# Layer norm with tokens on partitions in the attention stage of a four-layer network

## The chip, the cores and the metric

The kernel runs on one core of a Trainium2 chip. The metric is the device time of one execution in microseconds (us). A core has a matrix engine (PE, with weight loads listed as PEld), a vector engine (DVE), an activation engine (ACT), a general engine (POOL) and a queue that issues transfers (SP). Each works through its own instructions in order, and they wait for each other through semaphores. Matrix products are written to PSUM, eight banks of 2 KB per partition.

## The reference, cut to what matters

Four layers follow each other: a Mamba block, a depthwise convolution with a GELU network, a linear attention with a quantised network, and a Fourier layer with a quantised network. The change lies in layer 2 and at the start of layer 3. There are 4 images of 4096 tokens with 96 channels.

```
t = t + attn(ln(t))            # layer 2
t = t + ffn_quantised(ln(t))
t = t + fourier(ln(t))         # layer 3
t = t + ffn_quantised(ln(t))

def ln(v):                     # over the 96 channels of a token
    return (v - mean(v)) / sqrt(var(v) + 1e-5)
```

The attention has no softmax, so for a head it is q (k^T v) with biases. A batch therefore needs the Gram matrix of its normalised tokens (with a row of ones for the biases), from which one 97x96 matrix follows, by which every token is multiplied.

## The kernel before

The stream `t` stays in SBUF as [96 channels, 16384 tokens] in float32. Function `layer2` works on blocks of 512 tokens (MB), 8 per batch (NB), n = 32 in all. It writes the order of all its instructions by hand: one loop over iterations j, in which each step handles a block that is some iterations behind. Nothing is reordered later, so what stands first in an iteration is first in its engine's queue.

There are 72 blocks to normalise: 0 to 31 for the attention, 32 to 63 for the quantised network (FFN), and 64 to 71 for the first batch of the Fourier layer, written to `h3`. All go through `norm_steps`. Step `center` multiplies by a centring matrix (L1084, to PSUM tile `xc_ps`) and squares the result on ACT (L1086). Step `scale` multiplies the squares by a matrix of ones (L1090, tile `v_ps`), which sums them over the channels and leaves the sum on all partitions, and takes Ln and Exp on ACT (L1092, L1093). Step `norm` multiplies on DVE (L1096).

For the attention, `turn` then transposes a normalised block in four pieces of 128 tokens (L1131) and ACT copies them to SBUF (L1133); `products` adds them to the Gram matrix (L1141). At the end of a batch, `weights` gives five small steps: copies on ACT, small products on PE (L1147) and a mask on DVE (L1165). They are handed out over the following iterations, two at a time. Step `out` multiplies a block by the batch's matrix (L1179) and adds to `t` on DVE (L1181), 15 iterations after the block was centred.

The FFN steps `hidden` (three products L1236, three ACT copies L1238, three DVE operations L1239, a POOL cast L1240) and `project` (L1246, two DVE operations L1248 and L1250, a POOL addition L1252) run in the same loop, three and five iterations after the block is centred. The tile of `project` shares its PSUM bank with that of `out`.

The loop's core, with the order within an iteration:

```python
lag = NB + 3
for j in range(2 * n + NB + 2):
    scale(j - 1); center(j)
    norm(j - 2, ...)
    products(j - 4)        # at a batch's end: steps = weights(b)
    turn(j - 3)
    for f in steps[:2]: f()
    out(j - 4 - lag)
    project(j - n - 5)
    hidden(j - n - 3)
```

Two neighbours of the change appear in the text because they do similar things. Layer 1 normalises with tokens on partitions: DVE statistics (L1006, L1007), Ln and Exp on 16 values per partition (L1011, L1012), DVE scaling (L1020), transposes back (L1025). Layer 0 does so with ACT operations (L371, L377, L378, L384), transposes L390 and copies L401. In the Fourier layer, L1376 is an ACT operation with a scale and a bias per partition, read from PSUM. L594, L488 and L940 are transposes on PE in layers 0 and 1.

Of the kernel before, what the change touches and what calls it, by code (L numbers as in the profile page):

```python
# [9 lines left out]
F32 = mybir.dt.float32  # L10
# [3 lines left out]
AF = mybir.ActivationFunctionType  # L14
ALU = mybir.AluOpType
# [3 lines left out]
B, C, HW, L = 4, 96, 64, 4096  # L19
NT = B * L  # L20
T = 1024
NSC = L // T
MB = 512
# [79 lines left out]
class Net:  # L103
# [972 lines left out]
    def norm_steps(self, t, wk, psum):  # L1076
# [20 lines left out]

        return center, scale, norm

    def layer2(self, t, h3):
        tc, nc = self.tc, self.nc
        NB = L // MB
        n = B * NB
        engines = {mybir.EngineType.PE, mybir.EngineType.DVE, mybir.EngineType.Activation, mybir.EngineType.Pool}
        with ExitStack() as ctx:
            wk = ctx.enter_context(tc.tile_pool(name="l2w", bufs=1))
            psum = ctx.enter_context(tc.tile_pool(name="l2p", bufs=1, space=PSUM))
            tc.keep_in_program_order(nc.scalar.preload_act_table_set(ACT_EXP_LN))  # L1110
            ctx.enter_context(tc.manual_schedule(engines=engines))
            center, scale, norm = self.norm_steps(t, wk, psum)
            hidden, project, xq = self.ffn_steps("f2", t, wk, psum, ("ht", "gram", "small", "o"))
            nc.gpsimd.memset(h3[C:], 1.0)

            hs = []
            for k in range(2):
                h = wk.tile([C + 1, L], F32, name=f"h{k}")
                nc.gpsimd.memset(h[C:], 1.0)
                hs.append(h)  # L1120
            ht, gram, g = {}, {}, {}

            def block(i):
                b, s = divmod(i, NB)
                return hs[b % 2][:, s * MB : (s + 1) * MB]

            def turn(i):
                h = block(i)
                ps = psum.tile([128, 4, C + 1], F32, name="ht_ps", tag="ht")
                for d in range(4):  # L1130
                    nc.tensor.transpose(ps[:, d], h[:, d * 128 : (d + 1) * 128], self.ident[: C + 1, : C + 1])  # L1131
                ht[i] = wk.tile([128, 4, C + 1], F32, name="ht", tag="hts", bufs=2)
                nc.scalar.copy(ht[i], ps)  # L1133

            def products(i):
                b, s = divmod(i, NB)
                if s == 0:
                    gram[b] = psum.tile([C + 1, C + 1], F32, name="gram", tag="gram")
                h = ht.pop(i)
                for d in range(4):  # L1140
                    nc.tensor.matmul(  # L1141
                        gram[b], h[:, d], h[:, d], start=s == 0 and d == 0, stop=s == NB - 1 and d == 3
                    )

            def small(w, x, rows, name):
                ps = psum.tile([C + 1, C], F32, name="small_ps", tag="small")[:rows]
                nc.tensor.matmul(ps, w, x, start=True, stop=True)  # L1147
                r = wk.tile([C + 1, C], F32, name=name, tag=name, bufs=2)[:rows]
                return r, ps

            def weights(b):

                m = {}

                def one():
                    m["g"] = wk.tile([C + 1, C + 1], F32, name="grams", tag="grams")
                    nc.scalar.copy(m["g"], gram.pop(b))

                def two():
                    m["p"], ps = small(m["g"], self.wkv[:, :C], C + 1, "gk")  # L1160
                    nc.scalar.copy(m["p"], ps)

                def three():
                    m["m"], ps = small(self.wkv[:, C:], m["p"], C, "kv")
                    nc.vector.tensor_mul(m["m"], ps, self.mask)  # L1165

                def four():
                    m["w"], ps = small(m["m"], self.wff, C, "mw")
                    nc.scalar.copy(m["w"], ps)

                def five():
                    g[b], ps = small(self.wqt, m["w"], C + 1, "g")
                    nc.scalar.copy(g[b], ps)

                return [one, two, three, four, five]

            def out(i):
                ps = psum.tile([C, MB], F32, name="o_ps", tag="o")
                nc.tensor.matmul(ps, g[i // NB], block(i), start=True, stop=True)  # L1179
                td = t[:, i * MB : (i + 1) * MB]  # L1180
                nc.vector.scalar_tensor_tensor(td, ps, self.v("bff"), td, ALU.add, ALU.add)  # L1181

            lag = NB + 3
            steps = []
            for j in range(2 * n + NB + 2):
                if 0 <= j - 1 < 2 * n + NB:
                    scale(j - 1)
                if j < 2 * n + NB:  # L1190
                    center(j)
                i = j - 2
                if 0 <= i < n:
                    norm(i, block(i)[:C])
                elif n <= i < 2 * n:
                    norm(i, xq(i - n), saturate=False)
                elif i >= 2 * n:
                    norm(i, h3[:C, (i - 2 * n) * MB : (i - 2 * n + 1) * MB])
                if 0 <= j - 4 < n:
                    products(j - 4)  # L1200
                    if (j - 4) % NB == NB - 1:
                        steps = weights((j - 4) // NB)
                else:
                    for f in steps[:1]:
                        f()
                    steps = steps[1:]
                if 0 <= j - 3 < n:
                    turn(j - 3)
                for f in steps[:2]:
                    f()  # L1210
                steps = steps[2:]
                if 0 <= j - 4 - lag < n:
                    out(j - 4 - lag)
                if 0 <= j - n - 5 < n:
                    project(j - n - 5)
                if 0 <= j - n - 3 < n:
                    hidden(j - n - 3)
# [464 lines left out]
```

## Time and profile before

| quantity | value |
|---|---|
| median of 4 runs | 3830.27 us (3827.86 to 3833.89) |
| profiled execution | 3833.89 us, span 3832.0 us |
| mean granted TensorE clock | 0.895 |
| busy: PE, DVE, ACT, POOL | 84%, 78%, 71%, 67% of the span |
| attention and its FFN, with the Fourier layer's first norm | 2923.6 to 3192.2 us, 268.6 us |
| of it, up to the first FFN block's iteration | 111.3 us |

The profiled execution is the slowest of the four, 3.6 us over their median. The shares are averages over stages with different limits: layer 0 alone takes the first two thirds of the span, and its POOL work says nothing on attention. So the stretch from 2923.6 us on is to be read by itself, in the windows by stage and in the timeline, where the start-to-start distances on one engine show what a step costs. PE's matrix products are pipelined, and the end of a product is modelled, so its listed duration is longer than its start-to-start distance. A float32 product over 512 columns is listed as two records.

### The profile page before, as it was taken

To read this page: it belongs to the slowest core of one execution; us is meant where nothing else is said; L and a number is where in the kernel's file an instruction comes from. 1 tells how busy PE (TensorE), PEld (TensorE's weight loads), DVE (VectorE), ACT (ScalarE), POOL (GpSimd) and SP (SyncE) were. 2 spreads that over 40 slices of the span, in tenths; PEclk is the share of its full clock that TensorE was granted. 3 is DMA by queue.
4 is the path that set the end of the run, shared out by engine and by line. 5 is a ranking of instruction groups with operands and counts; after the bars stand their busy time and mean duration, and the time that the engine had idled before them with its cause. 6 is when DMAs were issued, how large, how long until landed. Compare 5 with 4: busy or idle time off the path is not lost. (4 is left out here: it accounts for less than half of the span.)

```text
span 3832.0 us, 46555 instructions
## 1 busy us (share of the span) xinstructions
PE 3227.6 (84%) x15326; PEld 1474.3 (38%) x15326; DVE 2989.4 (78%) x2644; ACT 2718.9 (71%) x5456; POOL 2568.5 (67%) x922
## 2 busy tenths in 40 slices
PE   7888888888888888888888888657799998899988
PEld 3333333233323332333233323226544534666643
DVE  5999989999999999999999999952573384444649
ACT  6788788877887888778877887631345686666557
POOL 1988889888888898888888988832001064544527
PEclk8998899889998999899989887657899999999989
DMA  7566665656565656565666565556200000011101
GB/s 192 150 149 164 160 160 144 169 150 161 136 169 149 165 136 167 152 160 140 166 153 162 138 165 150 132 142 205 75 1 0 1 1 6 19 35 34 37 9 58
DMA packets 171642, 446.61 MB, mean 117 GB/s; under 512 B 48756, under 2 KB 50750, under 8 KB 168064
## 3 DMA queue, kind: packets, MB, share of 16 engines
q1 hardware_dynamic: 171400, 443.64, 44.6%
q8 instruction: 121, 1.98, 0.2%
q14 instruction: 121, 0.99, 0.1%
HBM read 369.97 MB, written 73.50 MB: 116 GB/s over the span
## 5 line engine op out<-in xcount | busy, mean ns | idle before, releaser
L648 POOL TENSOR_TENSOR hs<-hs,crep 128x2048 f32<-128x2048 f32 x384 | 1598.9, 4183 | 213.6 <-DVE hs L643 129.0
L610 ACT ACTIVATE da<-ddb,nega 128x1024 f32<-128x1024 f32 x576 | 657.7, 1147 | 191.9 <-DVE hs L643 181.5
L643 DVE TENSOR_TENSOR_SCAN hs<-da,state,rep 128x1024 f32<-128x1024 f32 x288 | 667.8, 2337 | 59.0 <-PE rep L594 42.9
L665 PE MATMUL y<-hs,sel_r 128*32 128x512 f32 x3072 | 458.2, 680 | 75.7 <-POOL hs L648 75.7
L621 POOL TENSOR_TENSOR up<-udb,brep 128x1024 f32<-128x1024 f32 x192 | 452.0, 2361 | 69.8 <-DMA udb<-ud 59.6
L594 PE MATMUL rep<-ident,uta 128*128 128x128 f32 x1536 | 244.9, 311 | 161.8 <-DVE hs L643 161.7
L507 ACT ACTIVATE uta<-delta,bt 128x192 f32<-128x192 f32 x1024 | 379.0, 442 | 1.1
L643 DVE TENSOR_TENSOR_SCAN hs<-dap,state,up 128x1024 f32<-128x1024 f32 x144 | 336.7, 2338 | 44.7 <-ACT dap L610 44.7
L643 DVE TENSOR_TENSOR_SCAN hs<-da,state,u 128x1024 f32<-128x1024 f32 x144 | 338.1, 2348 | 15.5 <-DVE u L636 0.5
L287 PE MATMUL ps<-n,w_x 97*64 97x512 f32 x1536 | 346.8, 599 | 1.5 <-ACT n L401 1.5
L594 PEld LDWEIGHTS rep<-ident,uta 128*128 128x128 f32 x1536 | 198.6, 159 | 268.0 <-DVE hs L643 148.0
L610 ACT ACTIVATE dap<-ddb,nega 128x1024 f32<-128x1024 f32 x192 | 214.0, 1115 | 102.0 <-DVE hs L643 101.4
L599 PE MATMUL rep<-dbl,sel_b 32*128 32x512 f32 x768 | 246.5, 720 | 29.7 <-DVE hs L643 28.7
L636 DVE TENSOR_TENSOR u<-udb,rep 128x1024 f32<-128x1024 f32 x192 | 235.7, 1228 | 39.4 <-DMA udb<-ud 13.7
L1240 POOL CAST hq<-y 128x1536 fp8e5<-128x1536 f16 x64 | 94.0, 1468 | 218.8 <-issue 122.6
L287 PE MATMUL ps<-dbl,dtw 103*64 103x512 f32 x384 | 172.9, 945 | 74.6 <-ACT dbl L441 74.6
L636 DVE TENSOR_TENSOR rep<-udb,rep 128x1024 f32<-128x1024 f32 x192 | 231.9, 1208 | 0.0
L643 DVE TENSOR_TENSOR_SCAN hs<-da,rep 128x1024 f32<-128x1024 f32 x96 | 216.8, 2277 | 15.0 <-PE rep L594 9.8
L665 PEld LDWEIGHTS y<-hs,sel_r 128*32 128x32 f32 x3072 | 68.5, 116 | 381.2 <-POOL hs L648 192.9
L287 PEld LDWEIGHTS ps<-n,w_x 97*64 97x64 f32 x1536 | 109.9, 137 | 232.4 <-issue 205.1
L479 POOL TENSOR_TENSOR delta<-delta,xc 128x1536 f32<-128x1536 f32 x31 | 106.5, 3437 | 93.1 <-DMA dd<-delta 80.0
L1379 POOL TENSOR_TENSOR av<-av,ec 128x780 f32<-128x780 f32 x32 | 58.8, 1836 | 133.2 <-ACT av L1376 133.2
(276 smaller groups left out, 6220.5 us busy)
## 6 DMA issues: line engine op xcount, KB each, us to landing
ddb<-dd SPq DMA_DIRECT2D x768, 128.0 KB
udb<-ud SPq DMA_DIRECT2D x768, 128.0 KB
crep<-cd SPq DMA_DIRECT2D x512, 128.0 KB
dd<-delta SPq DMA_DIRECT2D x64, 384.0 KB
band<-in_band SPq DMA_DIRECT2D x24, 1024.0 KB
ud<-delta SPq DMA_DIRECT2D x62, 384.0 KB
brep<-cd SPq DMA_DIRECT2D x128, 128.0 KB
x<-in_x SPq DMA_DIRECT2D x32, 384.0 KB
```

The source lines that it names most:

```text
L287: nc.tensor.matmul(ps[rows], w[:, 64 * p : 64 * p + 64], rhs[:, at.start + shift : at.stop + shift], start=k == 0, stop=k == len(ws) - 1, ...
L479: (nc.gpsimd if k else nc.vector).tensor_mul(m["du"], m["delta"], m["xc"])
L507: nc.scalar.mul(m["uta"][:, q, :, 32 * s4 : 32 * s4 + 32].rearrange("t (p j) d -> t p j d", p=3), m["udt"][:, :, q].rearrange("t p (j d) - ...
L594: nc.tensor.transpose(x[:, q * 128 : q * 128 + 128], made[k]["uta"][:, q, 2 * h + j], self.ident)
L599: nc.tensor.matmul(x[:, at], sel_b[rows, g], made[k]["dbl"][rows, at], start=True, stop=True)
L610: nc.scalar.activation(da, made[k]["dd", h, j], AF.Exp, scale=nega[:, col : col + 1])
L621: nc.gpsimd.tensor_mul(up, made[k]["ud", p][:, j], made[k]["brep", GP])
L636: nc.vector.tensor_mul(u, made[k]["ud", h][:, j], x)
L643: nc.vector.tensor_tensor_scan(hs[:, 1:], made[k].pop(("da", t)), u, st, ALU.mult, ALU.add)
L648: nc.gpsimd.tensor_mul(hs[:, :, :T], hs[:, :, 1:], twice(made[k]["crep", g]))
L665: nc.tensor.matmul(made[k]["y", p][row : row + 32], sel_r, made[k]["hs", p, g][:, j, at], start=False, stop=True, skip_group_check=True,)
L1240: nc.gpsimd.tensor_copy(q, y2, saturate=False)
```

## The change

For blocks 0 to 31 and 64 to 71 the norm is made with tokens on partitions, in a new function `token_norm`. Step `turn` transposes a block of `t` into PSUM in four pieces, and DVE takes mean and variance of each token (`bn_stats`, `bn_aggr`). Step `root` takes Ln and Exp on ACT of 4 values per partition, and minus mean times root on DVE. Step `times` scales and shifts on ACT from PSUM to an SBUF tile with tokens on partitions, whose column of ones is set once. Step `back` transposes it and copies the block on ACT to where the channels are on partitions. The Gram matrix is taken from the SBUF tile directly, so the former transposes of the normalised block and their copy go. Blocks 32 to 63 keep the old steps. `products` runs two blocks behind instead of four, and `out` 13 iterations after the block's first step.

```diff
+    def token_norm(self, wk, tile_of, back_of):
...
+        kept = [wk.tile([128, 4, C + 1], F32, name=f"nt{k}") for k in range(3)]
+        for k in kept:
+            nc.gpsimd.memset(k[:, :, C:], 1.0)
+        def turn(i, x):
+            ps = xt[i] = tile_of(i)
+            for d in range(4):
+                nc.tensor.transpose(ps[:, d], x[:, d * 128 : d * 128 + 128], self.ident[:C, :C])
+            m = mv[i] = wk.tile([128, 4, 2], F32, name="tmv", tag="tmv", bufs=3)
+            for d in range(4):
+                st = wk.tile([128, 6], F32, name="tst", tag="tst", bufs=4)
+                nc.vector.bn_stats(st, ps[:, d])
+                nc.vector.bn_aggr(m[:, d], st)
+        def root(i):
+            r = rs[i] = wk.tile([128, 2, 4], F32, name="trs", tag="trs", bufs=3)
+            nc.scalar.activation(r[:, 0], mv[i][:, :, 1], AF.Ln, bias=self.eps)
+            nc.scalar.activation(r[:, 0], r[:, 0], AF.Exp, scale=-0.5)
+            nc.vector.scalar_tensor_tensor(r[:, 1], mv.pop(i)[:, :, 0], -1.0, r[:, 0], ALU.mult, ALU.mult)
+        def times(i):
...
+            for d in range(4):
+                nc.scalar.activation(
+                    n[:, d, :C], x[:, d], AF.Identity, scale=r[:, 0, d : d + 1], bias=r[:, 1, d : d + 1]
+                )
+        def back(i, out):
+            ps = back_of(i)
+            for d in range(4):
+                nc.tensor.transpose(ps[:, d * 128 : d * 128 + 128], nt[i][:, d, :C], self.ident)
+            nc.scalar.copy(out, ps)
...
+            turn, root, times, back, ht = self.token_norm(
+                wk,
+                lambda i: psum.tile([128, 4, C], F32, name="xt_ps", tag="xc", bufs=3),
+                lambda i: psum.tile([C, MB], F32, name="tp_ps", tag=("v", "ht")[i % 2]),
+            )
-            def turn(i):
-                h = block(i)
-                ps = psum.tile([128, 4, C + 1], F32, name="ht_ps", tag="ht")
-                for d in range(4):
-                    nc.tensor.transpose(ps[:, d], h[:, d * 128 : (d + 1) * 128], self.ident[: C + 1, : C + 1])
-                ht[i] = wk.tile([128, 4, C + 1], F32, name="ht", tag="hts", bufs=2)
-                nc.scalar.copy(ht[i], ps)
-            lag = NB + 3
+            lag = NB + 5
-            for j in range(2 * n + NB + 2):
...
+            for j in range(total + 3):
                 i = j - 2
                 if 0 <= i < n:
-                    norm(i, block(i)[:C])
+                    back(i, block(i)[:C])
+                elif 2 * n <= i < total:
+                    a = (i - 2 * n) * MB
+                    back(i, h3[:C, a : a + MB])
+                if n <= j - 1 < 2 * n:
+                    scale(j - 1)
+                elif token_block(j - 1):
+                    root(j - 1)
+                if n <= j < 2 * n:
+                    center(j)
+                elif token_block(j):
+                    turn(j, t[:, j * MB % NT : j * MB % NT + MB])
+                if token_block(j - 1):
+                    times(j - 1)
+                if n <= i < 2 * n:
                     norm(i, xq(i - n), saturate=False)
-                if 0 <= j - 4 < n:
-                    products(j - 4)
...
+                if 0 <= j - 2 < n:
+                    products(j - 2)
...
-                if 0 <= j - 3 < n:
-                    turn(j - 3)
...
-                if 0 <= j - 4 - lag < n:
-                    out(j - 4 - lag)
+                if 0 <= j - lag < n:
+                    out(j - lag)
```

More of the change, by code (lines that the diff above doesn't have):

```diff
@@ L1098, in norm_steps @@
         return center, scale, norm
+    def token_norm(self, wk, tile_of, back_of):
+        nc = self.nc
+        xt, mv, rs, nt = {}, {}, {}, {}
+        kept = [wk.tile([128, 4, C + 1], F32, name=f"nt{k}") for k in range(3)]
[16 more added lines that the diff above has]
+        def times(i):
+            n = nt[i] = kept[i % 3]
+            x, r = xt.pop(i), rs.pop(i)
+            for d in range(4):
[7 more added lines that the diff above has]
+            nc.scalar.copy(out, ps)
+        return turn, root, times, back, nt
     def layer2(self, t, h3):
@@ L1120, in layer2 @@
                 hs.append(h)
-            ht, gram, g = {}, {}, {}
+            gram, g = {}, {}
+            turn, root, times, back, ht = self.token_norm(
[3 more added lines that the diff above has]
+            )
             def block(i):
@@ L1181, in out, with token_block @@
                 nc.vector.scalar_tensor_tensor(td, ps, self.v("bff"), td, ALU.add, ALU.add)
-            lag = NB + 3
+            lag = NB + 5
             steps = []
-            for j in range(2 * n + NB + 2):
[L1188 to L1191, printed above, removed]
+            total = 2 * n + NB
+            def token_block(i):
+                return 0 <= i < n or 2 * n <= i < total
+            for j in range(total + 3):
                 i = j - 2
                 if 0 <= i < n:
-                    norm(i, block(i)[:C])
-                elif n <= i < 2 * n:
-                    norm(i, xq(i - n), saturate=False)
-                elif i >= 2 * n:
-                    norm(i, h3[:C, (i - 2 * n) * MB : (i - 2 * n + 1) * MB])
-                if 0 <= j - 4 < n:
-                    products(j - 4)
-                    if (j - 4) % NB == NB - 1:
-                        steps = weights((j - 4) // NB)
+                    back(i, block(i)[:C])
[13 more added lines that the diff above has]
+                if n <= i < 2 * n:
+                    norm(i, xq(i - n), saturate=False)
+                if 0 <= j - 2 < n:
+                    products(j - 2)
+                    if (j - 2) % NB == NB - 1:
+                        steps = weights((j - 2) // NB)
                 else:
```

## The prediction

> **What bounds the kernel now.** I read the windows by stage first. The columns are PE, PEld, DVE, ACT and POOL busy (instructions), granted TensorE clock, DMA share and GB/s.
>
> ```profile
> 2923.60:3034.90 111.30, 104.19 (x524) 57.87 (x525) 31.80 (x49) 72.42 (x135) 6.22 (x2) 1.00 0.00 1
> 3034.90:3057.30 22.40, 21.09 (x94) 10.79 (x93) 9.75 (x19) 14.61 (x29) 1.46 (x1) 1.00 0.00 0
> 3057.30:3107.70 50.40, 40.74 (x122) 15.54 (x121) 39.28 (x69) 32.50 (x61) 26.32 (x20) 1.00 0.00 1
> 3107.70:3174.00 66.30, 64.63 (x198) 23.93 (x197) 64.26 (x117) 63.11 (x119) 50.83 (x39) 1.00 0.00 1
> 3174.00:3192.20 18.20, 12.29 (x28) 3.41 (x26) 10.05 (x18) 11.91 (x20) 6.43 (x5) 1.00 0.00 0
> ```
>
> The change touches these 268.6 us alone. Attention (first row) is PE's: 94% busy, DVE 29%. The quantised FFN (fourth row) is DVE's: 97%. The last row, the Fourier layer's first norm, is nobody's: a chain of latencies. Then the timeline of one attention iteration:
>
> ```profile
> 3003.91 1.02 PE L1090 MATMUL v_ps<-sq,ones 96*96 96x512 f32 x2
> 3004.11 0.75 DVE L1181 SCALAR_TENSOR_TENSOR t<-o_ps,vec,t 96x512 f32<-96x512 f32 x1 [2.25 <-PE o_ps L1179]
> 3004.77 1.02 PE L1084 MATMUL xc_ps<-t,center 96*96 96x512 f32 x2
> ...
> 3005.62 0.85 PE L1141 MATMUL gram<-ht 128*97 128x97 f32 x8
> ...
> 3006.31 0.50 PE L1131 MATMUL ht_ps<-ident,h 97*128 97x97 f32 x4
> 3006.64 1.02 PE L1179 MATMUL o_ps<-h,g 97*96 97x512 f32 x2
> ```
>
> Start to start: variance 0.86, centring 0.86, Gram 0.69, transposes 0.33, output 0.87. The next variance product starts at 3007.51, so an iteration is 3.60 us, all PE. Without the output product it is 3.01 (first batch, same view). A batch end (iterations of 4.73, 4.53 and 3.77) adds 2.2.
>
> Third, rows with the prices of what is added (timeline):
>
> ```profile
> 3310.70 3.63 ACT L1376 ACTIVATE av<-xr_ps,vec 128x65 f32<-128x65 f32 x12
> 11.13 1.97 ACT L384 ACTIVATE nt<-ps,rs 128x96 f32<-128x96 f32 x8
> 2836.18 0.31 DVE L1006 BATCH_NORM_STATS2 st<-xt 128x6 f32<-128x96 f32 x1
> 2836.53 0.18 DVE L1007 BATCH_NORM_AGGREGATE mv<-st 128x2 f32<-128x6 f32 x1
> 2836.62 0.29 DVE L1006 BATCH_NORM_STATS2 st<-xt 128x6 f32<-128x96 f32 x1
> ```
>
> An activation with a scale and a bias per partition (L1376) goes out every (3.63-0.41)/11 = 0.29 us at 65 columns; with a scale alone (L384), every 0.23 at 96. The third pair of stats starts 0.43 after the second, so four pairs take 1.70.
>
> Last, the clock, in windows that follow its steps of 3.41 us:
>
> ```profile
> 268.20:271.50 3.30, 1.64 (x13) 1.40 (x14) 3.30 (x3) 1.90 (x5) 2.24 (x1) 1.00 0.85 230
> 691.40:694.70 3.30, 1.77 (x20) 1.42 (x16) 3.30 (x3) 2.20 (x4) 2.51 (x1) 1.00 0.95 248
> 694.90:698.20 3.30, 3.03 (x12) 2.03 (x12) 3.30 (x2) 1.11 (x1) 3.30 (x2) 0.50 1.02 237
> 2548.20:2592.50 44.30, 19.47 (x103) 15.65 (x102) 24.80 (x27) 25.03 (x26) 0.00 (x0) 0.50 1.04 243
> 2749.70:2753.00 3.30, 3.05 (x7) 1.55 (x8) 2.66 (x11) 1.01 (x1) 0.00 (x0) 0.50 0.00 0
> 2753.10:2756.40 3.30, 3.30 (x9) 1.42 (x8) 3.13 (x15) 0.69 (x1) 0.00 (x0) 1.00 0.00 0
> 3237.70:3241.10 3.40, 1.58 (x6) 0.49 (x6) 2.44 (x3) 2.58 (x5) 3.00 (x2) 1.00 0.00 0
> 3241.10:3244.50 3.40, 3.40 (x7) 1.62 (x6) 1.80 (x2) 0.87 (x2) 3.40 (x4) 0.50 0.02 5
> ```
>
> A window with PE busy about half or less is followed by one at half clock (691, 3237); one almost full brings the clock back (2749, where transposes L1025 stand beside matmuls L1040). The window at 268 holds transposes alone, half busy, and the clock was still full in the next.
>
> **The change, part by part.** PE per iteration: the variance and centring products go (-1.72). The transposes to tokens stay (0.34, now from t), and four transposes back come in, 4 x 0.107 = 0.43 (L1025's pitch). With output: 3.60-1.72+0.43 = 2.31; without: 1.45. DVE: the product of norm (0.61) goes; stats 1.70 and one 128x4 operation (0.16 by L839's 128x3) come: with L1181's 0.75, 2.61. ACT: square, two 512-wide activations and the copy of 388 columns go; the copy back (0.48 start to start, as L401), Ln 0.34 and Exp 0.21 of 128x4 (as L377, L378) and four identities come. No engine has over 2.7 us of work, so PE stops being the bound.
>
> What is late next is a ring through ACT's queue. Its order per iteration is copy of block j-2, Ln, Exp, four identities of j-1. The copy waits for PE's transposes back, which wait for the identities at the end of the previous iteration. Identity pitch: L1376's 0.29 plus 31 columns x 0.82 ns (L401's 96x512 copy at 576 ns against L1169's 96x96 at 235) = 0.32; the last lasts 0.44. The ring: identities 3 x 0.32 + 0.44 = 1.40; to PE 0.05; last transpose to ACT 0.38 (in the Gram chain L1147 to L1161 takes 0.45 with one pass more); copy 0.48; Ln 0.34; Exp 0.21; to DVE and back with the 128x4 operation, 0.22. Sum 3.08. That is 0.52 under 3.60 and 0.07 over 3.01.
>
> Attention up to the first FFN block's iteration (32): before, 111.3 (first row). After: fill of four iterations 9 (PE waits there for the first block's stats, roots and identities, about 5 us; the three 128x4 memsets queue on POOL behind the two h rows, which end 6.2 us in, and the first Gram product waits for them, at most 1 us of these 9), 28 x 3.08 = 86.2, three batch ends. A batch end is dearer now: the Gram copy stands on ACT behind the identities, the first small product on PE waits for it, and output and transposes back are queued behind that product: +1.5. An iteration later the mask's product on DVE stands behind four stats and PE waits again: +1.7. Thus 3 x 3.2 = 9.6. Total 104.8: **-6.5**.
>
> Iterations 32 to 46: outputs come two iterations earlier (13 after the turn, not 15). An FFN iteration that carries an output takes 5.03 (the y_ps and o_ps tiles share a bank), one without 3.3 or less. Before: 3 x 3.60 + 4.83 + 5.02 + 4.92 + 9 x 5.03 = 70.8; after: 3.6 + 5.1 + 4.2 (the last batch end), 2 x 3.3 before the first projection, 8 x 5.03, 2 x 3.2 = 66.1. **-4.7**. The 17 FFN iterations after that are unchanged, at DVE's 3.45.
>
> The Fourier layer's first batch costs. Its first three blocks run beside FFN work on DVE, which is full. From the DVE product at 3167.08 to the last block at 3192.20: 25.1. After, DVE per iteration: 0.61+1.17+1.69+1.70 = 5.17; with the 128x4 operation 5.33; without the product 4.72; then four of the ring's 3.08; and from the last block's stats to its copy 1.70+0.04+0.34+0.21+0.22+1.40+0.43+0.57 = 4.9. Sum 32.4: **+7.3**. What follows (loading the table, w1) starts from the copy as it did from the DVE product; nothing here.
>
> At full clock that is -3.9. **The clock** comes on top. The first window has two turns, 0.68 of 3.41: half clock follows, as after 3237. At half clock, PE's 2.9 without output still hides, but the last transpose and its latency add some 0.15 to the ring, up to 11 x 0.15 = 1.6; I take 0.7. At a batch end PE works 2.5 of about 5.2 us, the share at which the rows go either way; a drop then makes the next iterations PE's, 4.62 instead of 3.08, until a window is full. About one such iteration per batch end, 3 x 1.54 = 4.6. Together 5.3; from both sides 0, if no drop is long, to 11, at two iterations each. I take the middle, since 691 and 3237 are the nearest to a batch end. The Trainium skill ("TensorE: Matmul & The Clock Gate", "Part 4: PE-mode transpose") speaks against the change: transposes do not count as PE work for releasing the clock. The row at 268 disagrees about keeping the clock; the transposes at 2548 are too thin to tell; by the page alone the sum would be that of the second rival.
>
> Sum: -6.5-4.7+7.3+5.3 = +1.4. The profiled execution took 3833.89 (span 3832.0 and 1.9 around it), the slowest of four; on it, 3835.3; on the median 3830.27, 3831.7, so I say 3832. Open prices: stats read PSUM now. L270's copy from PSUM (96 columns, 253 ns) is no dearer than L247 from SBUF (258), while L1020 with its stride, as L1006's, costs 351. So pairs of 0.40 to 0.50; at 0.50 +2.4, at 0.40 -1.
>
> **The rivals.** First, faster: the identities go at L384's 0.23 and end at 0.36. The ring is 2.73, which saves 0.35 in some 28 iterations and six of the tail: 1.4-12 = -10, 3820. For it: same shape, also PSUM. Against: L1376 has both operands, as here. It decides once the pitch is under 0.25.
>
> Second, slower: the clock stays at half after its fall in the first window, because half of the non-output PE work is transposes. Each output iteration is then 4.62: 19 x 1.54 = +29 in place of 4.6, thus about +26; if it holds for half of them, +11. For it: 2548 to 2592, where transposes alone ran at half clock throughout. Against: 2749, which came back with a mixture like this one. It decides from four iterations at half clock on.
>
> Third: the change does not act. Not so: in its instruction order the two products are gone from PE in these blocks. What can be left is that the terms cancel, which is my forecast.
>
> **How the numbers follow.** What a measurement of this kernel can tell from no change is about 0.2%, 7.7 us. Forecast case 0.57 (of it 0.05 faster by more than that, 0.07 slower, 0.45 same); clock at half 0.26, all slower; cheap identities 0.15, all faster; no action 0.02, same. Faster 0.20, same 0.47, slower 0.33. The range 3818 to 3849 takes in the first rival, the clock's 0 to 11, the stats' bounds and the second rival up to +19.
>
> **What would show it.** Right: iterations of 3.1 us in attention with ACT waiting for tp_ps; 5 us at batch ends; windows at 0.50 clock after 2927 and after batch ends; DVE full from FFN block 59 on, and h complete some 7 us later after the last FFN block's iteration. Wrong: identities at 0.23, stat pairs over 0.50, PE at half clock through whole batches.

## The result, and the profile after

The changed kernel took 3835.01 us (median of 33 runs), the kernel before 3831.36 beside it (53 runs): a ratio of 1.0008, 95% interval 1.0003 to 1.0014. That is 3.65 us slower, under the 0.2% named in the prediction. The profiled execution took 3833.36 us, span 3831.5.

The two traces are best laid on each other from the end of layer 1's last DVE operation (L1043: 2923.58 us before, 2918.84 after; what lies ahead of it is the same code, and its 4.7 us are scatter). From there:

| us from the end of layer 1 | before | after | step's own difference | predicted |
|---|---|---|---|---|
| product L1096 of the first FFN block (32) | 119.41 | 118.39 | -1.0 | +0.3 (-6.5, +5.3 for the clock, +1.5) |
| the same, FFN block 44 | 179.66 | 174.01 | -4.6 | -4.4 |
| the same, FFN block 61 | 240.04 | 232.62 | -1.8 | -1.8 |
| last block of h complete | 268.61 | 271.54 | +10.3 | +7.3 |
| end of the kernel | 908.44 | 912.66 | +1.3 | 0 |

The product of block b stands in iteration b + 2. So the +1.5 that the prediction has for iterations 32 and 33 (8.7 for 7.2) falls into the first row here, and its -4.7 for iterations 32 to 46 becomes -6.2 for the second and third row.

Now the timeline of one attention iteration of the kernel after (start, duration, engine, line, tiles, count, and in brackets idle time and who ended it). The new steps are L1110 (transposes to tokens), L1114 and L1115 (statistics), L1119 to L1121 (root), L1127 (the four identities), L1134 and L1135 (transposes back and copy); L1217 is the former L1181.

```profile
2989.56 0.58 ACT L1135 COPY h<-tp_ps 96x512 f32<-96x512 f32 x1 [0.40 <-PE tp_ps L1134]
...
2990.05 0.30 ACT L1119 ACTIVATE trs<-tmv,eps 128x4 f32<-128x4 f32 x1
...
2990.37 0.21 ACT L1120 ACTIVATE trs<-trs 128x4 f32<-128x4 f32 x1
...
2990.81 1.40 ACT L1127 ACTIVATE nt<-xt_ps,trs 128x96 f32<-128x96 f32 x4 [0.23 <-DVE trs L1121]
...
2991.29 1.28 PE L1134 MATMUL tp_ps<-ident,nt 128*96 128x128 f32 x4
...
2992.61 0.58 ACT L1135 COPY h<-tp_ps 96x512 f32<-96x512 f32 x1 [0.41 <-PE tp_ps L1134]
```

Copy to copy is 3.05 us, and every part is a link: copy 0.49, Ln 0.32, Exp and DVE's turn 0.44, identities 1.40, and 0.40 in which ACT waits for the transposes back. The kernel before had PE working without a gap there (3.60); now no engine is full.

The windows of the kernel after, the whole stretch up to the first FFN block first, then steps of the clock (PE, PEld, DVE, ACT, POOL busy, granted clock, DMA share, GB/s):

```profile
2918.90:3037.20 118.30, 101.76 (x588) 67.07 (x589) 62.74 (x312) 81.11 (x242) 6.36 (x5) 0.87 0.00 1
2918.86:2922.27 3.41, 0.88 (x8) 0.70 (x8) 1.90 (x12) 0.79 (x3) 3.41 (x2) 1.00 0.00 0
2922.27:2925.68 3.41, 2.44 (x10) 1.65 (x11) 1.72 (x11) 2.61 (x9) 2.99 (x4) 0.50 0.00 0
...
2946.16:2949.58 3.42, 1.57 (x17) 1.41 (x16) 1.51 (x9) 2.66 (x9) 0.00 (x0) 1.00 0.00 0
2949.58:2952.99 3.41, 2.75 (x17) 2.51 (x16) 1.65 (x10) 2.42 (x8) 0.00 (x0) 0.50 0.02 5
2952.99:2956.40 3.41, 3.41 (x21) 3.38 (x22) 0.96 (x6) 2.05 (x7) 0.00 (x0) 0.50 0.00 0
```

The mean clock of the stretch fell from 1.00 to 0.87. The clock halves after the first window (PE 0.88 of 3.41) and after each of the first three batch ends (2946: 1.57 of 3.41), and here comes back after a full window (2952). That a full window brings it back is not so everywhere: in the kernel before, PE was busy for 3.40 of 3.40 us from 3193.30 on at 0.50, and the next window was still at 0.50. In the window at 2952, transposes are listed for 1.75 of PE's 3.41 us (0.85 to tokens, 1.11 back, 0.21 of it both at once), and the clock came back all the same.

Last, the tail, in which the Fourier layer's first batch is normalised beside the last FFN blocks. L1298 and L1286 are POOL's addition and cast for the FFN:

```profile
3158.18 1.74 POOL L1298 TENSOR_TENSOR t<-t,z 96x512 f32<-96x512 f32 x1 [1.57 <-DVE z L1296]
3158.81 2.54 DVE L1121 SCALAR_TENSOR_TENSOR trs<-tmv,trs 128x4 f32<-128x4 f32 x1
3159.87 1.46 POOL L1286 CAST hq<-y 128x1536 fp8e5<-128x1536 f16 x1
...
3173.33 1.15 POOL L1298 TENSOR_TENSOR t<-t,z 96x512 f32<-96x512 f32 x1 [1.07 <-DVE z L1296]
3173.62 0.88 DVE L1121 SCALAR_TENSOR_TENSOR trs<-tmv,trs 128x4 f32<-128x4 f32 x1 [0.37 <-ACT trs L1120]
```

DVE's operation on 4 values per partition, 0.16 us in attention, takes 2.54 here, and ends within 0.02 us of POOL's cast (3161.35 and 3161.33). The second slow one, 0.88, ends within 0.02 us of POOL's addition (3174.50 and 3174.48), and so does a third of 0.74 at 3177.52. The three cost 3.7 us that the prediction did not have.

### The profile page after: what moved, and what is told of

It reads as the page before. It is cut to its first block, busy times and chain, and to the rows that moved or that the text cites. A ratio compares the mean times of both kernels' runs of the same rounds, so it can differ in the third digit from the quotient of the medians.

```text
span 3831.5 us, 47077 instructions
## 1 busy us (share of the span) xinstructions
PE 3217.3 (84%) x15358; PEld 1483.2 (39%) x15358; DVE 3023.8 (79%) x2964; ACT 2727.0 (71%) x5584; POOL 2569.7 (67%) x925
## 5 line engine op out<-in xcount | busy, mean ns | idle before, releaser
L1286 POOL CAST hq<-y 128x1536 fp8e5<-128x1536 f16 x64 | 93.9, 1467 | 212.1 <-DVE y L1285 206.4
```

What stands on the lines that cost most here:

```text
L1286: nc.gpsimd.tensor_copy(q, y2, saturate=False)
```

## The experiments

My theory: attention gains what the sum says, its period is the ring through ACT, the clock's drops take part of it back, and the tail takes back the rest. The rivals stand with each run. All ratios are against the kernel before, run beside.

**e1: the token norm for the attention alone.**

```diff
-                return 0 <= i < n or 2 * n <= i < total
+                return 0 <= i < n
...
-                if n <= j < 2 * n:
+                if n <= j < total:
                     center(j)
...
+                elif 2 * n <= i < total:
+                    norm(i, h3[:C, (i - 2 * n) * MB : (i - 2 * n + 1) * MB])
```

> The token norm stays for the attention's 32 blocks; the Fourier layer's first batch (blocks 64 to 71) goes back to centring, ones product and DVE product. Theory A (the changed kernel gives its gain in attention back in the tail after the last FFN blocks: 34.0 us from the last FFN norm to the last h, where the kernel before took 25.1): the tail returns to 25 to 27 us, the kernel is 7 to 9 us faster than the changed one and about 4 to 5 us faster than the kernel before, near 3827. Rival B (the tail costs nothing, since the loading of the next stage hides it, and the changed kernel's loss lies in attention): within 1 us of the changed kernel.

Measured: 3822.49 us, ratio 0.9976 (0.9967 to 0.9985), 12 us under the changed kernel. From the product of FFN block 62, the last but one, to the last h it takes 25.12 us, before 25.11, after 33.98. Theory A holds, rival B falls: the tail's cost is not hidden. Of the 3 to 5 us beyond the expectation, 4.2 are seen ahead of that stretch. 1.5 lie between the products of blocks 61 and 62, which take 3.45 here, as in the kernel before, and 4.93 in the kernel after: the tail's cost begins one iteration earlier than the expectation has it. And 2.7 lie in attention: the first FFN block's product starts at 115.69 for 118.39, with the same attention code. Two of the three batch ends have only one window at 0.50 in this run, against two and three in the kernel after: where a step of the clock falls against a batch end changes from run to run and moves the stretch by 2.7 us. The trace of e4 below, again with the same attention code, has nine windows at 0.50 like the kernel after, and its first FFN product at 118.32.

**e2: Ln and Exp ahead of the copy.**

```diff
             for j in range(total + 3):
                 i = j - 2
+                if n <= j - 1 < 2 * n:
+                    scale(j - 1)
+                elif token_block(j - 1):
+                    root(j - 1)
                 if 0 <= i < n:
                     back(i, block(i)[:C])
...
-                if n <= j - 1 < 2 * n:
-                    scale(j - 1)
-                elif token_block(j - 1):
-                    root(j - 1)
```

> One reorder of the loop: Ln and Exp of block j-1 are issued ahead of the transposes back and the copy of block j-2, so that ACT's order is Ln, Exp, copy, identities. Theory A (the period of 3.05 us is a ring through ACT: identities, transposes back, copy, Ln, Exp, identities, in which ACT waits 0.40 us for the transposes): Ln and Exp fill that wait and the copy falls out of the way; the period goes to 2.4 to 2.7 us, ACT's own work, and the kernel is 18 to 28 us faster than the changed one, near 3810. Rival B (the period is DVE's work, 2.6 us of it, with its own latencies): 2.9 to 3.05 us stay, 0 to 5 us. Rival C (PE's work at a clock that falls more often): the period falls where the clock is full, and the windows at 0.50 become more; under 10 us.

Measured: 3807.74 us, ratio 0.9937 (0.9925 to 0.9950): 27 us under the changed kernel, 24 under the one before. The timeline of an iteration:

```profile
2989.20 0.30 ACT L1119 ACTIVATE trs<-tmv,eps 128x4 f32<-128x4 f32 x1
...
2989.53 0.21 ACT L1120 ACTIVATE trs<-trs 128x4 f32<-128x4 f32 x1
...
2989.64 0.56 ACT L1135 COPY h<-tp_ps 96x512 f32<-96x512 f32 x1
...
2989.80 0.15 DVE L1121 SCALAR_TENSOR_TENSOR trs<-tmv,trs 128x4 f32<-128x4 f32 x1
...
2990.11 1.39 ACT L1127 ACTIVATE nt<-xt_ps,trs 128x96 f32<-128x96 f32 x4
...
2991.52 0.30 ACT L1119 ACTIVATE trs<-tmv,eps 128x4 f32<-128x4 f32 x1
```

The period is 2.32 us, a little under the 2.4 to 2.7 expected, and no ACT line has a wait in brackets any more: DVE's turn lies beside the copy, and the transposes back beside Ln and Exp. Not an operation was taken away, so the 0.73 us per iteration were latency in the ring and nothing else. Rival B falls: DVE's work is the same. Rival C falls too: no batch end has a window at 0.50 now. Where the kernel after had PE busy for 1.57 and 1.95 us of a batch end's window, the two windows here from 2994.50 on have 2.29 and 2.46 of 3.41.

Not all of the 27 us is the period. In the traces the first FFN product comes 26.2 us earlier than in the kernel after (92.16 for 118.39): 28 periods give 20.4 of it, the batch ends most of the rest, about 5. The tail is 4.3 shorter as well. What sets the 2.32 is not shown: ACT starts one operation behind the other, and PE is busy for 7.00 of 7.00 us from 2987 on.

**e3: products that keep the clock.**

```diff
+            def fill():
+                ps = psum.tile([C, MB], F32, name="fill_ps", tag="small")
+                nc.tensor.matmul(ps, self.ones, t[:, 31 * MB : 32 * MB], start=True, stop=True)
...
+                if j == 0 or j == 1:
+                    fill()
+                    fill()
...
                     if (j - 2) % NB == NB - 1:
+                        fill()
+                        fill()
...
+                    elif j > 10 and (j - 2) % NB == 0:
+                        fill()
```

> Products of ones with a block of t, whose result nobody reads, are added on PE where it is idle in attention: two after each of the first two turns, two after the Gram products at each batch's end, one in the iteration after. Theory A (the half-clock windows at the start and at the batch ends cost the 5 us that the prediction's clock term says): the windows at 0.50 between 2922 and 3015 us go, and the kernel is 3 to 5 us faster than the changed one. Rival B (at half clock PE's work hides in the ring, so the drops cost nothing): the windows go and the time stays within 1 us, or up to 3 us slower where the added products stand ahead of small products or transposes.

Measured: 3831.98 us, ratio 1.0002 (0.9993 to 1.0011). This interval and the changed kernel's overlap, so the times alone do not decide; the trace does. The window of the stretch up to the first FFN block:

```profile
2915.70:3031.00 115.30, 104.89 (x617) 61.71 (x618) 62.89 (x313) 80.98 (x242) 6.34 (x5) 0.99 0.00 1
```

The mean clock is 0.99, and the stretch is 3.0 us shorter. One window at 0.50 is left of nine, at the first batch end: the condition `j > 10` leaves out the added product in the iteration after it. The tail did not change (33.97 us). The 3.0 hold a loss. In iteration 32 ACT's copy begins 4.7 us earlier than in the kernel after (105.63 for 110.37, counted as in the table). At the fourth batch end, where the kernel after had no window at 0.50, the added products cost 1.6: the interval between two outputs is 6.58 there for 4.95. So up to iteration 32 the drops cost at least 4.7 us: rival B, that they hide, falls, and theory A's 3 to 5 holds.

**e4: no DVE operation with two SBUF tensors in the tail.**

```diff
-            nc.vector.scalar_tensor_tensor(r[:, 1], mv.pop(i)[:, :, 0], -1.0, r[:, 0], ALU.mult, ALU.mult)
+            if i < 32:
+                nc.vector.scalar_tensor_tensor(r[:, 1], mv.pop(i)[:, :, 0], -1.0, r[:, 0], ALU.mult, ALU.mult)
+            else:
+                m = mv.pop(i)
+                for d in range(4):
+                    nc.vector.tensor_scalar(
+                        r[:, 1, d : d + 1], m[:, d, 0:1], r[:, 0, d : d + 1], -1.0, ALU.mult, ALU.mult
+                    )
```

> For the Fourier layer's first batch alone, the 128x4 operation on DVE with two SBUF tensors (minus mean times root, L1121) becomes four tensor_scalar operations of 128x1 each, with the root as a per-partition operand. Theory A (the three slow executions of L1121 in the tail, 2.5, 0.9 and 0.7 us where 0.16 is usual, wait for POOL's use of SBUF while POOL adds and casts): the slow ones go, the four operations cost 0.3 to 0.5 us per block in their place, and the kernel is 1 to 3.5 us faster than the changed one. Rival B (they wait for something else, such as DVE's own earlier work): slow ones stay at one of the four operations, and the time is the same or up to 2 us longer.

Measured: 3832.73 us, ratio 0.9999 (0.9991 to 1.0008); this too overlaps the changed kernel's interval. In the timeline of the tail (lines are 7 further on: L1305 is POOL's addition, L1126 the new operation):

```profile
3161.93 1.72 POOL L1305 TENSOR_TENSOR t<-t,z 96x512 f32<-96x512 f32 x1 [1.57 <-DVE z L1303]
3162.55 0.57 DVE L1126 TENSOR_SCALAR trs<-tmv,trs 128x1 f32<-128x1 f32 x4
3163.59 1.46 POOL L1293 CAST hq<-y 128x1536 fp8e5<-128x1536 f16 x1
```

In the middle of POOL's addition the four operations take 0.57 together, as in all eight blocks (0.56 to 0.58). None is slow, so rival B falls: it was the form with two SBUF tensors that waited for POOL. (POOL's addition takes 1.72 here and 1.15 to 1.19 where nothing holds it; the three DVE operations of `hidden`, here the y passes, go ahead of it, as the last section tells.) The tail went from 33.98 to 29.48 us. That is more than the 3.7 of the stalls less what the longer operations cost. Part of it is seen: in two of the last FFN iterations the y passes take 0.87 together where they took 1.80 and 1.77, because none is caught behind POOL's addition (see the last section). The rest of the 4.5 us is not split by this run.

**e5: the edits of e1 and e2 together.**

> Both earlier edits at once: Ln and Exp ahead of the copy, and the token norm for the attention's blocks alone. Theory A (the ring and the tail are separate costs): the gains add. The reorder gave 27 us against the changed kernel and the tail 9 of the 12.8 that e1 gave; with the reorder the tail is already 4.3 us shorter (29.6 for 34.0), so 4.5 us are left of it: about 3802 to 3804. Rival B (the tail's cost is hidden once the attention is shorter, or the reorder's gain depended on it): within 1 us of the reorder alone, 3808.

Measured: 3799.99 us, ratio 0.9914 (0.9899 to 0.9929). That is 2 us under the 3802 to 3804 expected, and 7.8 under e2 where 4.5 were counted on; 1.5 of the difference is again the iteration of block 62 (3.45 for 4.93), and the rest is within the interval. The stretch from block 62's product is 25.12 us again, and the intervals between outputs in attention are those of e2 (2.32). Ring and tail are separate costs and their removal adds up; rival B falls.

**e6: identities without the bias.** It leaves out the subtraction of the mean.

```diff
-                    n[:, d, :C], x[:, d], AF.Identity, scale=r[:, 0, d : d + 1], bias=r[:, 1, d : d + 1]
+                    n[:, d, :C], x[:, d], AF.Copy, scale=r[:, 1, d : d + 1]
```

> The four activations of times scale only (Copy with a scale per partition, no bias), which leaves out the subtraction of the mean; all else is the changed kernel. Theory A (the ring, of which three pitches of 0.32 and the last activation are a part; the price of the second operand is what the prediction's first rival turned on): the pitch goes from 0.32 to 0.23, the ring from 3.05 to 2.7 and the kernel is 8 to 14 us faster than the changed one. Rival B (the pitch is set by the 96 columns from PSUM, not by the second operand): pitch and time stay within 1 us.

Measured: 3824.20 us, ratio 0.9977 (0.9967 to 0.9987), 11 us under the changed kernel. The groups by line, after and then e6 (busy, mean ns of one):

```profile
L1127 ACT ACTIVATE nt<-xt_ps,trs 128x96 f32<-128x96 f32 x41 | 14.4, 430 | 2.3 <-DVE trs L1121 2.3
```

```profile
L1127 ACT ACTIVATE nt<-xt_ps,trs 128x96 f32<-128x96 f32 x48 | 12.4, 341 | 2.7 <-DVE trs L1121 2.7
```

Four take 1.40 us with the bias and 1.03 without, a pitch of (1.40-0.43)/3 = 0.32 against (1.03-0.34)/3 = 0.23. The period goes from 3.05 to 2.68, by just these 0.37. So the link is on the ring at full length: theory A. The edit also changes the function, from Identity to Copy. That the operand is the price and not the function is seen in layer 1 of the kernel before, where L993 is an Identity with a bias alone, read from PSUM:

```profile
2603.20 1.14 ACT L993 ACTIVATE xt<-cv_ps,cb 128x128 f32<-128x128 f32 x4 [9.00 <-PE cv_ps L986]
```

One lasts 0.37, so its pitch is (1.14-0.37)/3 = 0.26 at 128 columns; less 32 columns x 0.82 ns it would be 0.23 at 96, an estimate that meets e6's. The prediction's choice between L1376 (both operands) and L384 (scale alone) was the right question.

**e7: batch ends spread out, on top of e5.** The two traces had shown why a batch end is dear. In e2 (rows of PE's weight loads at the first small product and at the third):

```profile
2996.31 0.25 PEld L1183 LDWEIGHTS small_ps<-wkv,grams 97*97 97x97 f32 x2 [1.28 <-ACT grams L1193]
...
3000.17 0.24 PEld L1183 LDWEIGHTS small_ps<-wff,kv 96*96 96x96 f32 x2 [1.12 <-DVE kv L1201]
```

PE stands 1.28 us for a copy queued behind the identities, then 1.12 for the mask's product queued behind the statistics, and output and transposes back stand behind PE.

```diff
+                if len(steps) == 2:
+                    steps.pop(0)()
                 if token_block(j - 1):
                     times(j - 1)
...
                     if (j - 2) % NB == NB - 1:
                         steps = weights((j - 2) // NB)
-                else:
-                    for f in steps[:1]:
-                        f()
-                    steps = steps[1:]
-                for f in steps[:2]:
+                for f in steps[:1]:
                     f()
-                steps = steps[2:]
+                steps = steps[1:]
```

> On top of e5: the five small steps of a batch end are handed out one per iteration, behind the Gram products, the fourth between the transposes to tokens and the identities; output stays 13 iterations behind. Theory A (a batch end costs 3.2 us in the reordered kernel since the small products wait on PE for copies that stand behind the identities, and output and the transposes back wait behind them): the two intervals of 3.85 us between outputs at each batch end go to 2.4 to 2.7, the kernel is 5 to 8 us faster than e5. Rival B (a batch end costs what its own copies and products take, wherever they stand): 0 to 2 us faster.

Measured: 3791.07 us, ratio 0.9894 (0.9878 to 0.9909), 8.9 us under e5. The same step in e7's timeline:

```profile
2987.57 0.25 PEld L1183 LDWEIGHTS small_ps<-wff,kv 96*96 96x96 f32 x2
...
2988.43 0.25 PEld L1183 LDWEIGHTS small_ps<-mw,wqt 96*97 96x97 f32 x2
```

No wait stands there. The intervals between outputs at a batch end are 2.50, 2.49 and 2.66 in place of 3.85, 3.85 and 2.49, and the first FFN block comes 7.4 us earlier than in e5 (84.90 for 92.29). Theory A; the 8.9 are a little over the 5 to 8 expected, and these 7.4 are what the trace shows of them. This is the fastest version: 40 us, 1.1%, under the kernel before.

## Why the prediction was right, and where its terms were off

The time of 3832 was 3 us under the measured 3835; 1.1 of that is the kernel before itself (3831.36 here, 3830.27 then). The reading behind it held: two gains and two losses of like size. The change is +3.65 us for the +1.4 summed. Its interval lies above no change, so it is a small loss, under the 0.2% that the prediction took for the limit of a measurement. That the sum came so close is in part luck: the terms below are off by up to 3 us, in both directions.

**The ring: right, link by link.** 3.08 was summed, 3.05 measured, and e2 and e6 show that it is the period: e6 shortens a link by 0.37 and the period falls by 0.37, and e2 takes nothing away but the waiting.

**Attention to iteration 32: right in the sum, by errors that cancel.** Summed were 104.8 us and 5.3 for the clock, 110.1; iteration 32's copy began at 110.37. The fill was undersized: iteration 4's copy was due 9 us in and began at 12.02, and at 11.54 in e3, so 2.5 of it are not the clock: the first copy, in iteration 2, begins 5.45 in there, and iterations 2 and 3 already take a period of 3.05 each. The others were oversized. The ring gave 28 x 0.03 = 0.8. The first three batch ends took 8.7 in e3 for the 9.6 summed (3.4 each where outputs run, from 4.87 and 4.64 for two periods of 3.05, but 1.9 at the first, which has none). The clock cost 4.7, as e3 shows, for 5.3.

**Iterations 32 and 33, the last batch end: oversized.** 8.7 was summed; from iteration 32's copy to the start of iteration 34 it is 7.15.

**Outputs two iterations earlier: right.** From there to block 61 it is -6.4 for -6.2.

**The tail: right in sign and mechanism, undersized.** +10.3 for +7.3. Two steps of the sum failed. It starts at the product of block 62, and in that iteration (64) the statistics of block 64 already stand ahead of the product on DVE. The kernel after:

```profile
3151.46 0.68 DVE L1096 TENSOR_TENSOR xq<-xc_ps,rs 96x512 fp8e5<-96x512 f32 x1
...
3154.91 0.25 DVE L1114 BATCH_NORM_STATS2 tst<-xt_ps 128x6 f32<-128x96 f32 x1
...
3156.39 0.66 DVE L1096 TENSOR_TENSOR xq<-xc_ps,rs 96x512 fp8e5<-96x512 f32 x1
```

It is 4.93 from product to product, where the iteration before takes 3.45: 1.5 that the sum put at nothing. The other step is "with the 128x4 operation 5.33", which takes its 0.16 from L839 in another layer. The prediction looked at DVE's occupation in the tail and not at what POOL does beside it; the stalls add 3.7. The first iteration shows it: from one L1121 to the next 7.48 us, which is the 2.38 of the stall and 5.10, against 5.33 summed. The statistics gave some back: a pair takes 0.37, where 0.43 was summed and 0.40 to 0.50 allowed for (232 ns for L1114 from PSUM, where 310 and 290 stood for L1006), 0.24 per iteration. The Trainium skill has the rule that was missed ("SBUF — State Buffer", section "SBUF: two separate sides"): a VectorE operation with two SBUF inputs and a GpSimd operation that reads SBUF exclude each other, and whichever starts first holds the shared pair of ports for its whole length. This tail and e4 agree with it: the three slow L1121 run beside a POOL operation and end just after it, the other five run beside none.

**What follows the tail: no sign of a loss.** The stretch from the last h to the end took 641.1 for 639.8. With the same code there it took between 639.4 (e7) and 645.2 (e6) in the other profiles, so the +1.3 is within that scatter.

**The rivals.** The first, cheap identities, needed a pitch under 0.25 and met 0.32; e6 shows that its price per iteration was right (0.37 for 0.35). That the whole agrees too (11 us under the changed kernel, where it said 12 under the forecast) is in part luck: in the trace attention is 13.8 shorter, 10.4 of it the period and most of the rest the batch ends, with three windows at 0.50 for nine, and the stretch behind h took 4.1 longer. The second, a clock that stays at half, needed four output iterations at 0.50. The longest drop in attention was three windows (3004 to 3014), and after the window at 2952, about half transposes, the clock was back. Layer 0 of the kernel after has a window of transposes alone (eight of L390, four of L488), and the clock came back after it as well:

```profile
58.49:61.90 3.41, 2.96 (x12) 2.01 (x12) 0.00 (x0) 3.38 (x13) 0.00 (x0) 0.50 1.03 233
61.90:65.31 3.41, 2.15 (x9) 0.94 (x11) 1.23 (x1) 3.38 (x11) 2.35 (x1) 1.00 1.06 236
```

So here transposes do count for the clock, against the sentence of the Trainium skill ("TensorE: Matmul & The Clock Gate", "Part 4: PE-mode transpose") that the prediction weighed.

## What to carry to other kernels

When the busiest engine is relieved and none takes its place, walk the chain of queues once around and sum it: here the order of three instructions in ACT's queue was worth seven times the whole change. Price a moved operation with what the other engines do at its new place, above all POOL beside DVE operations with two SBUF tensors. And try a change stage by stage: this one is about 12 us of gain and 15 us of loss, and only the sum is next to nothing.

## What the runs showed of the hardware that was not expected

- **DVE waiting for POOL on tiny operations.** All slow L1121 of the runs (0.74 to 2.54 us) end 0.013 to 0.021 us after an operation of POOL; where POOL's cast follows its addition at once, DVE waits for both.
- **The same in the FFN, also before the change.** A y pass of 128x512 f16 on DVE (L1239 before) takes 0.34 us, but in most FFN iterations one of the three takes 1.24 and ends 0.15 us after POOL's addition (in the kernel before at 3169.11, with POOL's addition from 3169.01 to 3170.20). In the tail of e4 the same passes went ahead of the addition, which then took 1.72 in place of 1.19. Some 0.9 us of the FFN's 3.45 us iteration are this wait, but what its removal would bring is open, and so is what decides who goes first; no run tried. Once in the kernel after, at 3111.89, the three passes took 0.86 and the iteration 2.55; in the next one L1296 took 1.26 in place of 0.47 and the iteration 4.25, so that the two together were only 0.1 shorter.
- **A second operand per partition on ACT** costs 0.09 us per activation at 128x96 (pitch 0.32 with scale and bias, 0.23 with the scale alone).
- **The steps of the clock are not tied to the program.** Three traces hold the same attention code. The first FFN product came at 118.39 and 118.32 us where nine windows were at 0.50 (the kernel after, e4), and at 115.69 where six were (e1), because the batch ends fell differently against the windows.
